# Weight scaling moved from VectorE and ScalarE to GpSimd, and layer 3 of one sample given a shorter share of the schedule, in a four-layer attention network

## The chip, the cores and the metric

The kernel runs on one core of a Trainium2 chip. A core has five engines, each with an instruction queue of its own that is worked off in order: TensorE (PE, matrix products and transposes, with its weight loads listed as PEld), VectorE (DVE), ScalarE (ACT), GpSimd (POOL) and SyncE (SP, which here only issues DMAs). They meet through semaphores. The metric is the device time of one execution in microseconds, as the median of several runs.

## The reference

An input of 16 samples, 64 x 64 tokens of 256 channels, float32, goes through four residual layers. Before each, a group norm over 32 groups of 8 channels is taken, over all tokens of a sample.

```
x = x + L0(gn(x))   # nearest of 1024 code vectors, by distance; the code is added
x = x + L1(gn(x))   # f, g, h = three projections (32, 32, 256 wide); rows of 64 tokens:
                    # out = sigmoid(f g^T) h
x = x + L2(gn(x))   # three projections to one number per token (x0, x1, x2);
                    # sm = softmax over n of x0[n] * x1[m]; gate = sigmoid(x2 . sm);
                    # gate * x
x = x + L3(gn(x))   # linear attention, 4 heads of 32: softmax of q over the head's width,
                    # of k over the tokens; context = k v^T; projection, bias, layer norm
```

A group norm is an affine map of each channel, so its factor can be multiplied into the rows of the next weight, and its mean goes into a bias row. These are the scalings that the change is about.

## The kernel before

Each sample passes through six stages, written as Python generators that yield after small steps:

- `stats0`: statistics of the input for the first norm.
- `stage1`, the search: for each of 32 tiles of 128 tokens PE makes the products with all codes (`pd`, L403), DVE adds the norms and takes the maximum in one instruction (L409), finds its place (L414), and GpSimd adds the code's row by an indirect DMA, the gather (L415). Chunks of four tiles are then transposed back (L378).
- `layer1`: eight chunks of 512 tokens, projections `pfg` (L482) and `ph` (L493), scores, and the weighted sum `po` (L533), added on DVE (L538).
- `rows2`: the three projections of layer 2 to rows (`pr`, L593), written to DRAM and read back spread over all partitions (`x0b`, `x2b`).
- `stage2`, called exps in the schedule: 64 pairs of a 2048-wide exponential on ACT (`ex_s`, L645, with its sum) and a product with `x2b` and its sum on DVE (L648); both operands of the latter lie in the on-chip buffer SBUF. `gate2` then applies the gate (L702, L703).
- `stage3`: layer 3. For eight chunks the projections `pk` (L767) and `pqv` (L786), the running maximum of k (`nkm`, L770), the softmax of q with help of GpSimd (L808, L760), the context `pc` (L811, gathered on DVE in L813); then eight chunks of output with the variance (`pz` L863, `qz` L865), the deviation (`pdv`, `qo` L882) and the final products (L908 to L918).

The stages of neighbouring samples overlap. A list at the end of the kernel gives each stage of each sample a start and a length in units of one search, called a period here; a heap draws the generators' next steps by these times, and that order of recording is the priority. `LEN3` gives the length of layer 3 by the number of samples that come after (`left`); a sample not listed gets 1.0. A scheduler below then lays out each engine's queue from this order. Blocks under `tc.high_priority(offset=URGENT)` are pulled forward in it: the end of each norm and what hangs on it.

`gn_finish` (L276 and after) is the end of a norm: the groups' means on PE, squares and copies on ACT (L288, L293, L295), then on GpSimd the power of -0.5 (L296, on `scale`) and the product `nbias` (L298). For layer 2 a subtraction for a later layer (`xm_`, L688) stands before them in GpSimd's queue. What hangs on `scale`: in `layer1` the weights `wfg_n` (2 x 64 columns, ACT) and `wh_n` (2 x 256, DVE), then the bias products `pb` (L464) and `prow_h` (L163) on PE; in `rows2` two copies of 12 columns into `wrow_n` (ACT, L574), then PE's `pbr` (L579) and ACT's `brow_n` (L583); in `stage3` `wk_n` (2 x 128, ACT) and `wqv_n` (2 x 256, DVE), then `prow_qv` (L163). The helper `scaled` issues one instruction for each half of the channels, L306 on ACT or L308 on another engine.

Of the kernel before, what the change touches and what calls it, by code (L numbers as in the profile page):

```python
# [12 lines left out]
AF = mybir.ActivationFunctionType  # L13
ALU = mybir.AluOpType
AX = mybir.AxisListType

P = 128
# [17 lines left out]
LAG2 = 0.17  # L35
LAG3, LENG = 0.06, 0.8
LAG4 = 0.04
LEN3 = {0: 0.4, 1: 0.33, 2: 0.37}
FILL = ((0.05, 0.95, 2), (1.0, 1.27, 3), (1.4, 1.58, 2))
EARLY = sum(n for _, _, n in FILL)  # L40

# [2 lines left out]
def kernel(  # L44
# [7 lines left out]
    nc = tc.nc  # L52
# [17 lines left out]
    def bank(name):  # L70
        return ps_m.tile([P, 512], F32, tag="pm", name=name)
# [60 lines left out]
    def busy(t, n):  # L132

        for _ in range(n):
            nc.tensor.matmul(
                t[:, :512], lhsT=ones3, rhs=ones3.unsqueeze(1).to_broadcast([P, 4, P]), start=True, stop=True,
                skip_group_check=True,
            )
# [6 lines left out]
    def put_row(dst, v, weight, tag, plus=None, idle=0):  # L145

        v3 = small.tile([P, NK, PARTS], F32, tag="v3", name=f"v3_{tag}")
        nc.scalar.copy(v3, v.unsqueeze(2).to_broadcast([P, NK, PARTS]))
        pb = bank(f"prow_{tag}")
        busy(pb, idle)  # L150
        row = pb[:PARTS, :C]
        weight(row, v3, plus)

        for n in range(PARTS - 1):
            top = small.tile([PARTS, C], BF16, tag="ptop", name=f"top_{tag}_{n}", bufs=1)
            nc.scalar.copy(top, row)
            nc.tensor.matmul(row, lhsT=below[:, n, :], rhs=top, start=False, stop=True, skip_group_check=True)
        nc.scalar.copy(dst[0:PARTS, :], row)

    def by_weight(w):  # L160
        def make(out, v3, plus):
            for k in range(NK):
                nc.tensor.matmul(  # L163
                    out, lhsT=v3[:, k, :], rhs=w[:, k, :], start=(k == 0), stop=(plus is None and k == NK - 1),
                    skip_group_check=True,
                )
            for k in range(NK if plus is not None else 0):
                nc.tensor.matmul(
                    out[:, k * P : (k + 1) * P], lhsT=plus[:, k, :], rhs=ident, start=False, stop=(k == NK - 1),
                    skip_group_check=True,  # L170
                )
        return make
# [61 lines left out]
    wrow_raw = const.tile([P, NK, 4], F32, name="wrow_raw")  # L234
# [66 lines left out]
    def scaled(t, scale, engine):  # L301

        for k in range(NK):
            v = t[:, k]
            if engine is nc.scalar:
                nc.scalar.activation(v, v, AF.Copy, scale=scale[:, k : k + 1])  # L306
            else:
                engine.tensor_scalar(v, v, scale[:, k : k + 1], None, ALU.mult)  # L308
# [4 lines left out]
    def stats0(b):  # L313
        tag = f"s0_{b}"
        st = stats_tile(0, f"st_{tag}")
        src = xT[b].rearrange("(k p) n -> p k n", p=P)
        for ch in range(NCHUNK):
            xt = xb.tile([P, NK, CW], F32, tag="xb", name=f"xs_{tag}_{ch}")
            nc.sync.dma_start(out=xt, in_=src[:, :, ch * CW : (ch + 1) * CW])
            chunk_stats(st, xt, ch)  # L320
            yield 1.5
        with tc.high_priority(offset=URGENT):
            norm0[b] = gn_finish(st, "n0", b)
        yield 2
# [116 lines left out]
    def layer1(b):  # L441
        tag = f"l1_{b}"
        scale, nmean, _ = norm1.pop(b)
        x1 = x1_d.pop(b)
        wfg_n = wts.tile([P, NK, 2 * CK], F32, tag="wfg_n", name=f"wfg_{tag}")
        load_wfg(wfg_n)
        wh_n = wts.tile([P, NK, C], F32, tag="wh_n", name=f"wh_{tag}")
# [8 lines left out]
        load(1)  # L456
        with tc.high_priority(offset=URGENT):

            scaled(wfg_n, scale, nc.scalar)
            scaled(wh_n, scale, nc.vector)  # L460
            pb = bank(f"pb_{tag}")
            for n in range(4):
                for k in range(NK):
                    nc.tensor.matmul(  # L464
                        pb[n * CK : (n + 1) * CK, 0:1], lhsT=wfg_n[:, k, (n // 2) * CK : (n // 2 + 1) * CK],
                        rhs=nmean[:, k : k + 1], start=(k == 0), stop=(k == NK - 1),
                    )
            bfg_n = small.tile([P, 1], F32, tag="bfg_n", name=f"bfg_{tag}")
            nc.scalar.activation(bfg_n, pb[:, 0:1], AF.Identity, bias=bfg)
            put_row(h_row, nmean, by_weight(wh_n), f"h_{tag}", plus=bh3)  # L470
# [96 lines left out]
    def rows2(b):  # L567
        tag = f"r2_{b}"
        scale, nmean, _ = norm2[b]
        with tc.high_priority(offset=URGENT):  # L570
            pb = bank(f"pbr_{tag}")
            busy(pb, 3)
            for k in range(NK):
                nc.scalar.activation(  # L574
                    wrow_n[:, k, :].rearrange("p (j n) -> p j n", n=32)[:, :, 0:3],
                    wrow_raw[:, k : k + 1, 0:3].to_broadcast([P, 4, 3]), AF.Copy, scale=scale[:, k : k + 1],
                )
            for k in range(NK):
                nc.tensor.matmul(  # L579
                    pb[:, 0:1], lhsT=wrow_n[:, k, :], rhs=nmean[:, k : k + 1], start=(k == 0), stop=(k == NK - 1)  # L580
                )
            brow_n = small.tile([P, 1], F32, tag="brow_n", name=f"brow_{tag}")
            nc.scalar.activation(brow_n, pb[:, 0:1], AF.Identity, bias=brow)  # L583
        x01 = small.tile([P, NT, 2], F32, tag="x01", name=f"x01_{tag}", bufs=2)
        rd = dram.tile([3, 2, 4, CW], F32, tag="rows", name=f"rows_{tag}", bufs=3)
        for h in range(2):
            pr = bank(f"pr_{tag}_{h}")
            for j in range(4):
                xt = xb.tile([P, NK, CW], F32, tag="xb", name=f"xr_{tag}_{h}_{j}")
                nc.sync.dma_start(out=xt, in_=x2_d[b][4 * h + j])  # L590
                part = slice(32 * j, 32 * j + 32)
                for k in range(NK):
                    nc.tensor.matmul(  # L593
                        pr[part, :], lhsT=wrow_n[:, k, part], rhs=xt[:, k, :], start=(k == 0), stop=(k == NK - 1)
                    )
            rows = s1p.tile([P, CW], F32, tag="t4", name=f"rows_{tag}_{h}", bufs=3)
            nc.scalar.activation(rows, pr, AF.Identity, bias=brow_n)
            for n in range(3):
                nc.scalar.dma_start(out=rd[n, h], in_=rows[n : n + 97 : 32, :])
            pt = bank(f"prt_{tag}_{h}")  # L600
            for t in range(CH):
                nc.tensor.transpose(pt[:, t * P : (t + 1) * P], rows[:, t * P : (t + 1) * P], ident)
            nc.vector.tensor_copy(
                x01[:, 16 * h : 16 * h + 16, :].rearrange("p (j t) n -> p j t n", t=CH),
                pt.rearrange("p (t j n) -> p j t n", j=4, n=32)[:, :, :, 0:2],
            )
            yield 4
        rows_d[b] = x01, rd, [spread_rows(rd, b, 0)]

    def spread_rows(rd, b, h):  # L610

        x0b = s2p.tile([P, TOK // 2], F32, tag="x0b", name=f"x0b_{b}_{h}", bufs=2)
        x2b = s2p.tile([P, TOK // 2], F32, tag="x2b", name=f"x2b_{b}_{h}", bufs=2)
        for dst, n in ((x0b, 0), (x2b, 2)):
            nc.sync.dma_start(
                out=dst, in_=rd[n : n + 1, h, :, :].rearrange("o j n -> o (j n)").to_broadcast([P, TOK // 2])
            )
        return x0b, x2b
# [98 lines left out]
    def stage3(b):  # L717
# [3 lines left out]
        scale, nmean, xm_ = norm3.pop(b)  # L721
        wk_n = wts.tile([P, NK, P], F32, tag="wk_n", name=f"wk_{tag}")
        nc.sync.dma_start(out=wk_n, in_=w_src[:, :, 1, :])
        wqv_n = wts.tile([P, NK, 2 * P], F32, tag="wqv_n", name=f"wqv_{tag}")
        nc.sync.dma_start(out=wqv_n[:, :, 0:P], in_=w_src[:, :, 0, :])
        nc.sync.dma_start(out=wqv_n[:, :, P:], in_=w_src[:, :, 2, :])
        with tc.high_priority(offset=URGENT):
            scaled(wk_n, scale, nc.scalar)
            scaled(wqv_n, scale, nc.vector)
            put_row(qv_row, nmean, by_weight(wqv_n), f"qv_{tag}")  # L730
        yield 4

# [213 lines left out]
    def task(stage, ready, length, gen, total):  # L946
        start = max(ready, free.get(stage, 0.0))
        free[stage] = start + length
        tasks.append((start, length, gen, total))
        return start + length  # L950

    for b in range(nb):
# [9 lines left out]
        else:  # L962
            end = task("exps", end + LAG2, 0.65, stage2(b, NCHUNK), 200)
        task("layer3", end + LAG4, LEN3.get(left, 1.0), stage3(b), 160)
    for _ in stats0(0):
# [45 lines left out]
```

## Time and profile before

| what | value |
|---|---|
| median of three runs | 5653.41 us (5650.06 to 5654.34) |
| the profiled execution | 5630.88 us, span 5629.1 us |
| mean granted clock of PE | 0.964 |
| scalings on DVE (L308) | 64, 0.35 to 0.36 us each |
| scalings on ACT (L306) | 32 of wfg at 0.338 us, 32 of wk at 0.389 us |
| scalings on ACT (L574) | 32 at 0.294 us |
| GpSimd, busiest lines | gathers L415 1140.5 us, L808 249.7, L760 198.0, L874 172.3 |
| exps on DVE (L648) | 1024, mean 2.34 us |

Times in the views are microseconds from the first instruction of the profiled execution. A line of the timeline gives the start, the duration, engine, source line, operation, what it writes and reads with its shape, and in brackets how long the engine had been idle before it and what ended that. In the list for a source line the three numbers are the shortest, median and longest duration in ns, and below stand what its engine waited for (total us, times). Engines run ahead of each other through buffers, so an idle engine is a cost only where it is the one that the others wait for. The profiled execution is one of many and is 22.5 us shorter than the median of the runs.

### The profile page before, as it was taken

The page shows a single profiled execution, that of the slowest core. Times are in us where ns is not written, and L with a number is a line of the kernel's source. Part 1 is how long each engine was busy: PE and PEld are TensorE (multiplying, and loading weights), DVE is VectorE, ACT ScalarE, POOL GpSimd, SP SyncE. Part 2 cuts the span into 40 slices and gives each one's busy share as a digit, 9 for nine tenths or more (in the row PEclk, how much of TensorE's full clock was granted, in tenths as well). Part 3 has the DMA queues.
Part 4 walks back from the last instruction along what each step waited for, and adds up shares of the span by engine and source line. Part 5 has one row for each costly group of instructions (what it writes and reads, how often), then busy time and mean ns, then how long its engine had stood idle before and what let it go on. Part 6 is the DMA issues. An engine that isn't in the chain of part 4 may idle for free. (4 is left out here: it accounts for less than half of the span.)

```text
span 5629.1 us, 76169 instructions
## 1 busy us (share of the span) xinstructions
PE 5138.9 (91%) x26927; PEld 3174.3 (56%) x26927; DVE 5068.5 (90%) x7186; ACT 4560.2 (81%) x6642; POOL 1832.7 (33%) x1076
## 2 busy tenths in 40 slices
PE   7977989989999999999999999999999999997788
PEld 3533446545656556565655656565565656665566
DVE  7579789899999999999999999999999999988982
ACT  4468589788879888887988888798888979888873
POOL 2223223323333333433333343333334334321231
PEclk9988999999999999999999999999999999998889
DMA  8552744755665757566575756757575675745643
GB/s 253 173 184 73 227 132 123 226 166 174 192 214 150 235 156 228 184 204 221 164 251 152 230 175 207 228 155 247 154 226 183 204 226 152 231 152 193 203 158 121
DMA packets 521366, 1059.26 MB, mean 188 GB/s; under 512 B 52505, under 2 KB 266393, under 8 KB 512793
## 3 DMA queue, kind: packets, MB, share of 16 engines
q1 hardware_dynamic: 406288, 885.11, 46.9%
q0 software_dynamic: 73728, 67.14, 8.5%
q10 hardware_dynamic: 40968, 102.13, 4.7%
q8 instruction: 214, 3.51, 0.3%
q14 instruction: 168, 1.37, 0.1%
HBM read 751.18 MB, written 303.04 MB: 187 GB/s over the span
## 5 line engine op out<-in xcount | busy, mean ns | idle before, releaser
L648 DVE CUSTOM_DVE_ANT_0 ex_s<-ex_s,x2b 128x2048 f32<-128x2048 f32 x1024 | 2388.3, 2340 | 55.7 <-ACT ex_s L645 54.2
L645 ACT ACTIVATE ex_s<-x0b,nmax_s,x_r 128x2048 f32<-128x2048 f32 x1024 | 2138.5, 2089 | 40.3 <-DVE num_s L648 28.8
L403 PE MATMUL pd_s<-e,xn_s 128*128 128x512 f32 x4096 | 1971.2, 615 | 54.0 <-DVE m L409 41.8
L415 POOL DMA_INDIRECT xc_s<-in_emb_rows,i_s x512 | 1140.5, 2228 | 1778.4 <-DVE i_s L414 1274.6
L403 PEld LDWEIGHTS pd_s<-e,xn_s 128*128 128x128 f32 x4096 | 747.3, 196 | 786.9 <-issue 666.4
L409 DVE CUSTOM_DVE_ANT_0 nn_s<-pd_s,nn_s 128x1024 f32<-128x1024 f32 x512 | 620.1, 1213 | 114.4 <-PE pd_s L403 72.3
L414 DVE FIND_INDEX8 i_s<-m,nn_s 128x8 uint32<-128x1024 f32 x512 | 622.7, 1217 | 0.0
L398 ACT ACTIVATE nn_s<-ne,nx_s 128x1024 f32<-128x1024 f32 x512 | 583.3, 1145 | 40.7 <-DVE nx_s L369 24.8
L493 PE MATMUL ph_l<-wh_l,xt_l 128*128 128x256 f32 x2048 | 522.2, 392 | 33.8 <-DVE m L409 27.5
L786 PE MATMUL pqv_s<-wqv_s,xk_s 128*128 128x256 f32 x2048 | 489.3, 381 | 0.0
L493 PEld LDWEIGHTS ph_l<-wh_l,xt_l 128*128 128x128 f32 x2048 | 383.2, 194 | 144.9 <-issue 72.7
L786 PEld LDWEIGHTS pqv_s<-wqv_s,xk_s 128*128 128x128 f32 x2048 | 389.4, 191 | 120.7 <-issue 60.8
L808 POOL TENSOR_TENSOR qv_s<-qv_s,qm_s 128x512 f32<-128x512 f32 x128 | 249.7, 1951 | 580.6 <-DVE qm_s L807 316.0
L874 POOL TENSOR_TENSOR lrs_s<-lrs_s,mhalf 128x4 f32<-128x4 f32 x128 | 172.3, 1346 | 662.7 <-ACT lrs_s L873 655.3
L760 POOL TENSOR_TENSOR qv_s<-qv_s,qd_s 128x512 f32<-128x512 f32 x128 | 198.0, 1547 | 378.2 <-DVE qd_s L759 249.5
L378 PE MATMUL pt_s<-ident,xc_s 128*128 128x128 f32 x1024 | 163.0, 288 | 127.6 <-DMA xc_s<-in_emb_rows,i_s 102.3
L533 PE MATMUL po_l<-blk,h_l 128*128 128x128 f32 x2048 | 272.5, 282 | 3.2 <-DVE m L409 3.2
L533 PEld LDWEIGHTS po_l<-blk,h_l 128*128 128x128 f32 x2048 | 251.2, 194 | 36.8 <-issue 19.9
L914 PE MATMUL pxo_s<-wctx_s,qo_s 128*128 128x256 f32 x1024 | 267.8, 385 | 0.0
L767 PE MATMUL pk_s<-xk_s,wk_s 128*128 128x512 f32 x512 | 252.5, 616 | 1.4 <-DMA xk_s<-x_g 1.4
L378 PEld LDWEIGHTS pt_s<-ident,xc_s 128*128 128x128 f32 x1024 | 123.2, 147 | 191.7 <-DMA xc_s<-in_emb_rows,i_s 120.4
L919 ACT COPY y_s<-pxo_s 128x512 f32<-128x512 f32 x256 | 147.6, 580 | 103.2 <-PE pxo_s L918 102.4
(206 smaller groups left out, 7372.6 us busy)
## 6 DMA issues: line engine op xcount, KB each, us to landing
xs_s<-in_xT SPq DMA_DIRECT2D x128, 512.0 KB
xt_s<-in_xT SPq DMA_DIRECT2D x128, 512.0 KB
xc_s<-in_x SPq DMA_DIRECT2D x128, 512.0 KB
x_s<-xt_s ACTq DMA_DIRECT2D x128, 512.0 KB
xt_l<-x_s SPq DMA_DIRECT2D x128, 512.0 KB
x_l<-xt_l SPq DMA_DIRECT2D x128, 512.0 KB
xr_r<-x_l SPq DMA_DIRECT2D x128, 512.0 KB
xg_g<-x_l SPq DMA_DIRECT2D x128, 512.0 KB
```

What stands on the lines that cost most here:

```text
L378: nc.tensor.transpose(pt[:, t * P : (t + 1) * P], xc[ch][:, t, k * P : (k + 1) * P], ident)
L398: nc.scalar.activation(nn, ne2, AF.Identity, bias=nx2[ch][:, t : t + 1])
L403: nc.tensor.matmul(pd[:, cols], lhsT=xn[ch][:, k, t * P : (t + 1) * P], rhs=e2[:, k, cols], start=(k == 0), stop=(k == NK - 1),)
L409: nc.vector.tensor_tensor_reduce(out=nn, in0=pd, in1=nn, scale=1.0, scalar=-3.0e38, op0=ALU.add, op1=ALU.max, accum_out=m8[:, 0:1],)
L414: nc.vector.max_index(i8, m8, nn)
L415: nc.gpsimd.indirect_dma_start(out=xc[ch][:, t, :], out_offset=None, in_=emb_rows, in_offset=bass.IndirectOffsetOnAxis(ap=i8[:, 0:1], axis=0),
L493: nc.tensor.matmul(ph[:, t, :], lhsT=X[:, k, t * P : (t + 1) * P], rhs=wh_n[:, k, :], start=(t % 2 == 0 and k == 0), stop=False, skip_grou ...
L533: nc.tensor.matmul(po[:, m : m + P], lhsT=h[:, t, k * P : (k + 1) * P], rhs=at[:, t, :, :].rearrange("p r i -> p (r i)"), start=True, stop ...
L645: nc.scalar.activation(ex, x0b, AF.Exp, bias=nmax[:, T : T + 1], scale=x01[:, T, 1:2], accum_out=den[:, h, T : T + 1])
L648: nc.vector.tensor_tensor_reduce(out=ex, in0=ex, in1=x2b, scale=1.0, scalar=0.0, op0=ALU.mult, op1=ALU.add, accum_out=num[:, h, T : T + 1],)
L786: nc.tensor.matmul(pqv[:, j, :], lhsT=xt[:, k, t * P : (t + 1) * P], rhs=wqv_n[:, k, :], start=(j == 0 and k == 0), stop=False, skip_group ...
L914: nc.tensor.matmul(px[:, j, :], lhsT=qT[:, t * P : (t + 1) * P], rhs=wctx[:, 1, :], start=False, stop=False, skip_group_check=True,)
```

## The change

All weight scalings go to GpSimd, as one tensor-by-scalar product for each half of the channels; and the table of layer 3's lengths gets an entry for the thirteenth sample (three samples come after it), 0.7 of a period.

```diff
-LEN3 = {0: 0.4, 1: 0.33, 2: 0.37}
+LEN3 = {0: 0.4, 1: 0.33, 2: 0.37, 3: 0.7}
...
-            scaled(wfg_n, scale, nc.scalar)
-            scaled(wh_n, scale, nc.vector)
+            scaled(wfg_n, scale, nc.gpsimd)
+            scaled(wh_n, scale, nc.gpsimd)
...
-                nc.scalar.activation(
+                nc.gpsimd.tensor_scalar(
                     wrow_n[:, k, :].rearrange("p (j n) -> p j n", n=32)[:, :, 0:3],
-                    wrow_raw[:, k : k + 1, 0:3].to_broadcast([P, 4, 3]), AF.Copy, scale=scale[:, k : k + 1],
+                    wrow_raw[:, k : k + 1, 0:3].to_broadcast([P, 4, 3]), scale[:, k : k + 1], None, ALU.mult,
                 )
...
-            scaled(wk_n, scale, nc.scalar)
-            scaled(wqv_n, scale, nc.vector)
+            scaled(wk_n, scale, nc.gpsimd)
+            scaled(wqv_n, scale, nc.gpsimd)
```

What is computed stays the same. By the schedule's times layer 3 of that sample starts at 15.83 periods as before and ends at 16.53 and not at 16.83; the next sample's layer 3 starts at 16.83 in both.

## Prediction

> **What bounds the kernel now.** I read the page's busy line first, then busy time by stretch, then the groups of the scaling line, then the timeline around one sample's three scalings. The columns of the stretches are: from and to, length, then busy time and instructions of PE, PEld, DVE, ACT, POOL, then clock and DMA.
>
> ```profile
> PE 5138.9 (91%) x26927; PEld 3174.3 (56%) x26927; DVE 5068.5 (90%) x7186; ACT 4560.2 (81%) x6642; POOL 1832.7 (33%) x1076
> ```
> ```profile
> 4918.00:5076.00 158.00, 143.40 (x889) 103.04 (x888) 140.87 (x193) 138.32 (x214) 36.31 (x24) 0.95 0.48 154
> 5076.00:5200.00 124.00, 93.56 (x453) 61.42 (x454) 109.10 (x134) 100.74 (x144) 20.24 (x15) 0.85 0.57 199
> ...
> 1987.00:4951.00 2964.00, 2811.22 (x15128) 1751.35 (x15127) 2827.36 (x3985) 2548.89 (x3721) 1057.80 (x592) 0.99 0.64 199
> ```
>
> From 1987 to 4951 us (ends of the search's matmuls, L403, of the seventh and the sixteenth sample) nine samples pass, 329 us each. PE and DVE are both busy 95% of it (2811 and 2827 of 2964): they take turns in waiting for each other, so time freed on one counts only until the other ends the next wait. Later, in 4918 to 5200, where the change of layer 3's pace falls, PE goes from 91% to 75% while DVE stays at 88 to 89%.
>
> ```profile
> L308 DVE TENSOR_SCALAR wh_l<-wh_l,gn_s_n x32: 336/350/394, 193.2 to 4972.8; 128x256 f32<-128x256 f32 x32
> ...
>   POOL gn_s_n L296: 50.5, 31
> ```
>
> This line and its twin for wqv_s (x32, 0.36 us) are 64 scalings on DVE, and before 31 of the 32 pairs DVE sat idle for GpSimd's power of -0.5 (L296), 50.5 us in all. That looks like a prize of 50.5 + 64 x 0.35 = 73 us. The timeline says why it isn't.
>
> ```profile
> 3981.97 2.23 DVE L648 CUSTOM_DVE_ANT_0 ex_s<-ex_s,x2b 128x2048 f32<-128x2048 f32 x1
> 3982.03 3.07 POOL L808 TENSOR_TENSOR qv_s<-qv_s,qm_s 128x512 f32<-128x512 f32 x1 [6.87 <-issue]
> ...
> 3985.06 1.04 POOL L760 TENSOR_TENSOR qv_s<-qv_s,qd_s 128x512 f32<-128x512 f32 x1
> ...
> 3985.76 1.05 PE L811 MATMUL pc_s<-qv_s,ek_s 128*128 128x128 f32 x8
> ...
> 3986.84 0.65 DVE L308 TENSOR_SCALAR wh_l<-wh_l,gn_s_n 128x256 f32<-128x256 f32 x2 [2.63 <-POOL gn_s_n L296]
> ...
> 3987.41 0.34 DVE L813 SCALAR_TENSOR_TENSOR ctx_s<-ctx_s,al_s,pc_s 128x128 f32<-128x128 f32 x1
> ```
>
> Two things are to be seen. DVE's next instruction, L813, reads pc_s, whose matmuls end at 3986.81. And L808 and L760, the same shape on GpSimd, take 3.07 us when begun under ex_s (L648) and 1.04 us without: **GpSimd stands still while DVE runs ex_s.** The norm of the second layer shows the same at a two-column operation:
>
> ```profile
> 3904.33 2.28 DVE L648 CUSTOM_DVE_ANT_0 ex_s<-ex_s,x2b 128x2048 f32<-128x2048 f32 x1
> 3904.39 2.27 POOL L688 TENSOR_TENSOR xm_g<-bet,gn_nm_n 128x2 f32<-128x2 f32 x1 [1.28 <-ACT gn_nm_n L295]
> ...
> 3906.62 0.72 POOL L296 TENSOR_TENSOR gn_s_n<-gn_s_n,mhalf 128x2 f32<-128x2 f32 x1
> 3907.38 0.50 ACT L574 ACTIVATE wrow_n<-wrow_raw,gn_s_n 128x12 f32<-128x12 f32 x2 [2.03 <-POOL gn_s_n L296]
> 3907.43 0.19 POOL L298 TENSOR_TENSOR gn_nb_n<-gn_nm_n,gn_s_n 128x2 f32<-128x2 f32 x1
> 3907.75 2.27 DVE L648 CUSTOM_DVE_ANT_0 ex_s<-ex_s,x2b 128x2048 f32<-128x2048 f32 x1
> ```
>
> **Prices of the new instructions.** The trace has no scaling on GpSimd. Below, each costs what L298 costs with two columns, 0.19 us. Above, a line from L298 (0.19 at 2 columns) to the free L760 (1.04 at 512, two tensors read): 12 columns 0.21, 64 0.29, 128 0.40, 256 0.61. The new ones read one tensor, so the upper end is generous; I take it, as these are the same shapes. wfg and wh are then 2 x 0.29 + 2 x 0.61 = 1.8 us, wk and wqv 2.0, wrow 0.4 (lower ends 0.8, 0.8, 0.4). Any of them begun under ex_s waits up to 2.2 us more. Before them in GpSimd's queue stands L298 (0.19), behind them the gathers L415; the weights themselves are long there (the last wk load was issued at 5433.9, its scaling began at 5501.9). The Trainium skill (GPSIMD Engine Reference, Engine selection) advises against the move: ordinary elementwise work belongs on VectorE, though it grants GpSimd about the same rate where one tensor is read. Taken at that word the 256-column scaling would cost DVE's own 0.35 us in place of 0.61, the pairs 1.3 us at most, and the sum below would fall by 1 us or less; no run here shows which.
>
> **Layer 1's weights (wfg, wh), in a steady period.** Removed: DVE's 2.63 idle and 0.65 busy, ACT's 0.68 busy and 1.02 idle. In the order of the changed program L813 follows ex_s on DVE, waiting for PE's pc_s, ended at 3986.81: the same idle under another name. L813 starts near 3986.95 and not 3987.41: **0.46 us gained, not 3.3.** PE never paused there. The new scalings end near 3986.81 + 0.2 + 1.8 = 3988.8, or 3991 if the last is caught by an ex_s; PE wants wh at 3992.1 (L163, one matmul earlier in the new order than 3992.58). Covered; without that cover PE would wait. The gather behind them began at 3991.45: covered as well.
>
> **Layer 3's weights (wk, wqv).** In 1987 to 4951 PE takes them up more than 20 us after they are scaled, so the price on GpSimd is hidden (the next one there, near 3898, comes 11 us later). DVE gains its wait for L296 (5.0 us in seven samples of 2322 to 4633: 0.7) and 0.6 busy: **1.3 us**, on DVE alone.
>
> **Layer 2's rows (wrow).** Now the scalings stand behind L298 on GpSimd, which ends at 3907.62: the first runs to about 3907.8, the second meets the ex_s of 3907.75 and would end near 3910.1. PE's second L579 would wait till then in place of about 3907.95: **2.2 us lost** on PE (idle 1.72 us here already), on ACT (L583 waits for it, the exps behind) and on the rows, which the next sample's exps wait for. The phase is held, as L688 is released by the end of one ex_s and the next comes 1.21 us later; seven samples (2583 to 4566 us) show L688 at 2.27 us. Two more have L298 itself caught: I count nine.
>
> **Sum, steady.** Gains 12 x (0.46 + 1.3) = 21 us of DVE time, of which PE's part of the waits lets through half by my judgement: -11. Loss 9 x 2.2 = 20, on a chain that PE, ACT and the exps all hang on, seven tenths through: +14. Together **+3 us**.
>
> **Start.** At 499.6 and 747.3 the layer 1 chain has no cover: PE sat idle for it 1.3 and 0.9 us, and DVE has two ex_s next. Caught by both, the scalings come 4.4 us late; half through, twice: **+4 us**.
>
> **Layer 3 of sample 12.** Its start is unchanged (15.83 periods), its end goes from 16.83 to 16.53. The work is the same. I summed before's mean durations along both programs' orders: when its last deviation (L882) is done, DVE has 352 us left, against 318; PE's last pr_r (L593) has 342 against 373 left. So layer 3 is drawn into 4918 to 5076, where PE has 15 us to spare, and 5076 to 5200, with 30 to spare, gets emptier. DVE's work before the end of the next-to-last exps is the same, 286 us remaining against 287. The moved DMAs (layer 3's loads xk and xo and stores of y on SP, qT on ACT's queue) now pass the gate's loads of sample 13 and layer 1's of sample 15 on SP; the DMA engines are at 0.48 to 0.57 there, so I charge them nothing, and a late xt_l would cost its wait on PE, counted in the upper bound. For the pace itself I take 0, bounds -10 (most of DVE's 15 us of waits in 5076 to 5200 go) and +15 (PE's extra wait earlier is passed on in full). One consequence I do price: layer 3 of sample 13 now finds PE free, and DVE's first nkm (L770) stands 9.5 us of DVE work behind the norm, where it stood 39. Before that nkm come PE's statistics to pk, 7.4 us in before (5159.88 to 5167.27), 1.6 more on GpSimd, and the two casts that now precede pk, about 4: 13 us, without an ex_s in the way, and the DVE work there is nothing but ex_s. DVE waits 3.5 to 8: **+6 us** where DVE sets the end.
>
> **End.** Sample 15's wqv is on the path: pow to the end of the fourth prow_qv is 2.4 us now, later 0.2 + 2.0 + 0.9 = 3.1, +0.7. Sample 0's layer 1, with no exps yet and PE idle for it: wh ready 2.0 us after the power and not 0.7, +1.3. **+2 us.**
>
> Sum: 3 + 4 + 6 + 2 = +15. The profiled execution took 5630.9 us (span 5629.1); 5646. The median of the runs is 22.5 above it: **5668 us.** With the bounds of the pace, the largest unknown, its own range is 5658 to 5683.
>
> **Rivals.** *Faster (0.26):* the second wrow scaling slips in before ex_s and DVE's gains carry: 12 x -1.76 = -21, start and end +6, tail -10 + 3.5: 5632. For it speaks that 0.05 us decides; against, that ex_s follows ex_s wherever DVE is full. *Nothing (0.14):* gains and catches cancel, 5654: PE was busy at both weight changes. *Every scaling caught by its own ex_s (0.10):* four of wfg and wh take 9.2 us, against 5.3 of cover; 4 us of PE a period, 11 times, on top of the sum: 5712. Against it: at 3987 DVE has L813 and L409 first, and L808 ran its 1.05 us beside such work. It decides once DVE's ex_s come earlier than GpSimd's L296.
>
> **How the numbers follow.** Forecast 0.50, of which 0.09 lies within 0.2% (11 us, about what a measurement of this kernel can tell). Slower 0.41 + 0.10 = 0.51, same 0.09 + 0.14 = 0.23, faster 0.26. The range takes in the faster case's time and nearly the caught one's: 5628 to 5706.
>
> **What would show it.** Right: DVE's L813 idle for pc_s about 2.5 us a period; the second wrow scaling near 2.2 us and PE's L579 idle near 4; DVE idle at nkm near 5150 to 5180. Wrong: L308 and L574 on GpSimd all under 0.7 us with L579 idle under 2, or periods under 328 us; or PE waiting at prow_h_l, which makes the caught case.

## The result, and the profile after

The changed kernel took 5681.53 us (median of 14 runs, 5655.13 to 5707.56), the kernel before 5650.95 in the runs between them. The ratio is 1.0062 with a 95% interval of 1.0045 to 1.0079: **some 35 us slower** (25 to 45). All comparisons go by such ratios; the two medians alone differ by 30.6 us. One run of the kernel before took 8676 us and one of an experiment below 7092, and both stay out of the ratios. The forecast was 5668 us and slower, so its direction held and its size was too small. The profiled execution took 5670.3 us, 39 more than that of before.

The page's busy line of the changed kernel, and the stretches that answer to those of before (from and to, length, then busy time and instructions of PE, PEld, DVE, ACT, POOL, then granted clock, share of the DMA engines, GB/s). The third is again from the end of the seventh to the end of the sixteenth search, which lie at 1989.24 and 4986.58 now:

```profile
PE 5155.1 (91%) x26927; PEld 3187.3 (56%) x26927; DVE 5053.8 (89%) x7122; ACT 4537.5 (80%) x6546; POOL 1986.8 (35%) x1236
```
```profile
4918.00:5076.00 158.00, 143.90 (x790) 94.75 (x788) 129.22 (x189) 124.65 (x195) 49.73 (x31) 0.96 0.51 165
5076.00:5200.00 124.00, 99.44 (x607) 70.13 (x599) 103.46 (x120) 99.64 (x137) 27.45 (x19) 0.86 0.63 220
...
1989.24:4986.58 2997.34, 2836.56 (x15166) 1767.82 (x15165) 2823.45 (x3962) 2541.83 (x3679) 1137.22 (x685) 0.98 0.63 197
```

The nine steady samples take 2997 us and not 2964. DVE's work fell a little, as was wanted (2823 from 2827, though more of layer 3 lies within). PE is *busy* for longer, 2837 against 2811, and its granted clock went from 0.99 to 0.98. Not all of it is the 38 matmuls more: the search's own, of which there are as many in both stretches, show it in the groups of PE (busy us, mean ns of one, idle time before them), here before and after the change:

```profile
L403 PE MATMUL pd_s<-e,xn_s 128*128 128x512 f32 x2305 | 1100.5, 607 | 14.3 <-DVE m L409 12.8 <-DVE xt_l L538 1.5
L403 PE MATMUL pd_s<-e,xn_s 128*128 128x512 f32 x2305 | 1122.2, 617 | 12.6 <-DVE m L409 11.1 <-DVE xt_l L538 1.5
```

The same 2305 matmuls were busy for 1100.5 us, 607 ns each, and now take 22 us more for equal work. That is easily passed over; the experiments come back to it.

The groups of the two scaling lines after the change (shortest, median and longest ns):

```profile
L308 POOL TENSOR_SCALAR wfg_l<-wfg_l,gn_s_n x32: 432/444/2570, 192.1 to 5007.8; 128x64 f32<-128x64 f32 x32
L308 POOL TENSOR_SCALAR wh_l<-wh_l,gn_s_n x32: 912/917/2661, 193.0 to 5009.1; 128x256 f32<-128x256 f32 x32
L308 POOL TENSOR_SCALAR wk_s<-wk_s,gn_s_n x32: 592/606/2702, 790.2 to 5536.3; 128x128 f32<-128x128 f32 x32
L308 POOL TENSOR_SCALAR wqv_s<-wqv_s,gn_s_n x32: 912/917/4844, 791.3 to 5537.8; 128x256 f32<-128x256 f32 x32
L574 POOL TENSOR_SCALAR wrow_n<-wrow_raw,gn_s_n x32: 306/322/2422, 294.1 to 5149.7; 128x12 f32<-128x12 f32 x32
```

256 columns take 0.92 us where DVE took 0.35; the longest of each group are those begun under ex_s. And the timeline around layer 2's rows, at the sample that the prediction used (start, duration; in brackets the engine's idle time before):

```profile
3921.74 1.58 POOL L688 TENSOR_TENSOR xm_g<-bet,gn_nm_n 128x2 f32<-128x2 f32 x1 [0.75 <-ACT gn_nm_n L295]
...
3923.29 0.72 POOL L296 TENSOR_TENSOR gn_s_n<-gn_s_n,mhalf 128x2 f32<-128x2 f32 x1
3924.10 0.19 POOL L298 TENSOR_TENSOR gn_nb_n<-gn_nm_n,gn_s_n 128x2 f32<-128x2 f32 x1
3924.27 2.59 POOL L574 TENSOR_SCALAR wrow_n<-wrow_raw,gn_s_n 128x12 f32<-128x12 f32 x2
3924.40 2.28 DVE L648 CUSTOM_DVE_ANT_0 ex_s<-ex_s,x2b 128x2048 f32<-128x2048 f32 x1
...
3924.65 0.38 PE L579 MATMUL pbr_r<-gn_nm_n,wrow_n 128*128 128x1 f32 x2 [1.39 <-POOL wrow_n L574]
...
3926.92 0.38 PE L579 MATMUL pbr_r<-gn_nm_n,wrow_n 128*128 128x1 f32 x2 [1.89 <-POOL wrow_n L574]
...
3927.16 4.52 PE L403 MATMUL pd_s<-e,xn_s 128*128 128x512 f32 x6
3927.34 0.26 ACT L583 ACTIVATE brow_r<-pbr_r,brow 128x1 f32<-128x1 f32 x1 [4.75 <-PE pbr_r L579]
```

As forecast: the first scaling of 12 columns slips in (0.3 us), the second meets the ex_s of 3924.40, and the pair takes 2.59 us. PE waits twice and ACT 4.75 us. The waits over the nine samples (us in total, times, longest) show the same; the first line is of the kernel before, the others are of the changed one:

```profile
PE pbr_r L579 <- ACT wrow_n L574: 14.5, 9, 1.7
...
DVE ex_s L648 <- ACT ex_s L645: 50.7, 41, 3.8
ACT brow_r L583 <- PE pbr_r L579: 41.3, 9, 4.9
...
PE pbr_r L579 <- POOL wrow_n L574: 30.2, 17, 3.4
DVE nn_s L409 <- ACT nn_s L398: 28.1, 34, 3.1
DVE ctx_s L813 <- PE pc_s L811: 22.9, 16, 4.0
```

In the kernel before, PE waited 14.5 us there for wrow_n, DVE 29.7 for the exps of ACT and 16.4 for L398, and DVE's 23.7 us before the scaling of wh are now the 22.9 before L813.

### The profile page after: what moved, and what is told of

It is laid out like the page before. It is cut to its first block, busy times and chain, and to the rows that moved or that the text cites. A ratio compares the mean times of both kernels' runs of the same rounds, so it can differ in the third digit from the quotient of the medians.

```text
span 5668.6 us, 76211 instructions
## 1 busy us (share of the span) xinstructions
PE 5155.1 (91%) x26927; PEld 3187.3 (56%) x26927; DVE 5053.8 (89%) x7122; ACT 4537.5 (80%) x6546; POOL 1986.8 (35%) x1236
## 5 line engine op out<-in xcount | busy, mean ns | idle before, releaser
L648 DVE CUSTOM_DVE_ANT_0 ex_s<-ex_s,x2b 128x2048 f32<-128x2048 f32 x1024 | 2387.9, 2339 | 79.3 <-ACT ex_s L645 78.8
L403 PE MATMUL pd_s<-e,xn_s 128*128 128x512 f32 x4096 | 1990.1, 620 | 47.9 <-DVE m L409 35.4
L415 POOL DMA_INDIRECT xc_s<-in_emb_rows,i_s x512 | 1103.2, 2155 | 1705.5 <-DVE i_s L414 1245.3
L403 PEld LDWEIGHTS pd_s<-e,xn_s 128*128 128x128 f32 x4096 | 754.2, 197 | 785.8 <-issue 681.0
L398 ACT ACTIVATE nn_s<-ne,nx_s 128x1024 f32<-128x1024 f32 x512 | 583.2, 1145 | 39.4 <-DVE nx_s L369 24.0
L351 ACT ACTIVATE sq_s<-xt_s,first 128x512 f32<-128x512 f32 x256 | 200.1, 806 | 37.5 <-DMA x0b<-rows_r 24.1
```

The costliest lines, as they stand in the source:

```text
L398: nc.scalar.activation(nn, ne2, AF.Identity, bias=nx2[ch][:, t : t + 1])
L403: nc.tensor.matmul(pd[:, cols], lhsT=xn[ch][:, k, t * P : (t + 1) * P], rhs=e2[:, k, cols], start=(k == 0), stop=(k == NK - 1),)
L415: nc.gpsimd.indirect_dma_start(out=xc[ch][:, t, :], out_offset=None, in_=emb_rows, in_offset=bass.IndirectOffsetOnAxis(ap=i8[:, 0:1], axis=0),
L648: nc.vector.tensor_tensor_reduce(out=ex, in0=ex, in1=x2b, scale=1.0, scalar=0.0, op0=ALU.mult, op1=ALU.add, accum_out=num[:, h, T : T + 1],)
```

## The experiments

Each kernel was timed in turn with the kernel before on one chip. All ratios are to that kernel, whose median was 5640 to 5644 us there; 0.1% is 5.6 us. "Clock lost" is the mean over a kernel's runs of span x (1 - mean granted clock). It also counts the clock in stretches in which PE had nothing to do, so only differences of it are used.

| kernel | ratio | 95% interval |
|---|---|---|
| layer 3's length alone | 0.9999 | 0.9984 to 1.0015 |
| all scalings, old length | 1.0077 | 1.0056 to 1.0097 |
| wk and wqv alone | 0.9984 | 0.9971 to 0.9996 |
| layer 2's rows alone | 1.0065 | 1.0044 to 1.0085 |
| all scalings but the rows | 1.0010 | 0.9993 to 1.0026 |
| wfg and wh alone | 1.0028 | 1.0012 to 1.0044 |
| rows in one instruction | 1.0020 | 1.0006 to 1.0034 |
| rows, PE's second wait filled | 1.0045 | 1.0031 to 1.0060 |
| wk and wqv, PE's wait shortened | 0.9991 | 0.9975 to 1.0007 |
| wfg and wh from the fourth sample | 1.0008 | 0.9997 to 1.0019 |
| wfg and wh in the first three | 1.0021 | 1.0003 to 1.0040 |
| the change without its losing parts | 0.9973 | 0.9959 to 0.9987 |

### The change taken apart

The two traces had put 20 of the 39 us ahead of the last search and 16 more within it, where layer 3 of the thirteenth sample lies. That was read as a cost of the shorter length (theory A).

```diff
-LEN3 = {0: 0.4, 1: 0.33, 2: 0.37}
+LEN3 = {0: 0.4, 1: 0.33, 2: 0.37, 3: 0.7}
```

> The kernel before with only the new entry of 0.7 in the table of layer 3's lengths; every scaling stays on its old engine. Theory A (the loss in the tail, about 16 us between the start of the last search and its end, is the shorter layer 3 itself, drawn into a stretch where PE is full): +8 to +20 us on the kernel before, the last search some 10 us or more later. Rival (the pace costs nothing, and the tail only inherits late scalings): -5 to +5 us.

Measured: 0.9999, -1 us (-9 to +8). Of theory A's +8 to +20 only the lowest edge is left.

The same from the other side: the changed kernel with the table of before.

```diff
-LEN3 = {0: 0.4, 1: 0.33, 2: 0.37, 3: 0.7}
+LEN3 = {0: 0.4, 1: 0.33, 2: 0.37}
```

> All scalings on GpSimd, layer 3's lengths as in the kernel before. Theory A: the scalings are worth about +20 us, +15 to +28 with the end's wqv; the delay at the start of the last search (+20 us in the changed kernel) stays and does not grow to +36 behind it. Rival (the pace costs nothing): the whole +35 to +39 us. Rival (it is the pace alone): -5 to +5 us.

Measured: 1.0077, +43 us (32 to 55), no less than the whole change. The delay within the last search belongs to the scalings or to the one profiled execution, not to the length.

```diff
-            scaled(wk_n, scale, nc.scalar)
-            scaled(wqv_n, scale, nc.vector)
+            scaled(wk_n, scale, nc.gpsimd)
+            scaled(wqv_n, scale, nc.gpsimd)
```

> The kernel before with only wk and wqv scaled on GpSimd. Theory A (wk and wqv are wanted 20 us later, so that their price is hidden, and DVE and ACT gain): -10 to +2 us; of it about -12 in the steady part at most, +2 to +6 at the last sample, where wqv is on the path. Rival (each scaling on GpSimd costs what it is slower, 0.91 against 0.35 us for 256 columns, wherever it stands): 2 x 0.56 us a sample and its wait under ex_s, +10 us or more.

Measured: 0.9984, -9 us (-16 to -2). This part gains, though each scaling is slower: in the steady samples nobody waits for it. (Where PE does wait, at the fourteenth sample for 5.94 us and at the last for 3.32, the gain is larger than the loss.)

Then the rows alone: the two L574 on GpSimd as in the change, all else as before.

> The kernel before with only the layer 2 rows' two scalings (12 columns) on GpSimd. Theory A (the second is caught by ex_s, 2.2 us on PE, ACT and the rows): its duration about 2.3 us in a third of the 32 lines or more, PE's wait for wrow_n about 3.3 us a sample against 1.7, and +12 to +22 us. Rival (layer 1's weights are what costs the time, the rows are as fast on GpSimd, 0.31 us against 0.29 free): -3 to +5 us.

Measured: 1.0065, +37 us (25 to 48). **Two instructions of 12 columns a sample cost as much as the whole change.** That is also more than theory A's 12 to 22. PE waited 33.6 us at L579 over nine samples where it had waited 14.5: 2.1 us a sample, or 34 over all 16 if nothing of it were hidden.

### The catch

Both halves in one instruction, otherwise as the rows alone:

```diff
-            for k in range(NK):
-                nc.scalar.activation(
...
+            nc.gpsimd.tensor_tensor(
+                out=wrow_n.rearrange("p k (j n) -> p k j n", n=32)[:, :, :, 0:3],
+                in0=wrow_raw[:, :, 0:3].unsqueeze(2).to_broadcast([P, NK, 4, 3]),
+                in1=scale.unsqueeze(2).unsqueeze(3).to_broadcast([P, NK, 4, 3]), op=ALU.mult,
+            )
```

> The rows' scalings on GpSimd as in the run with them alone, but both halves in one instruction of 24 columns, so that no second one stands before ex_s. Theory B (the catch): the instruction takes 0.3 to 0.5 us in most samples, PE waits about 1.7 us a sample as before, time -4 to +8 us on the kernel before. Rival (it is the way over GpSimd, behind L298 in its queue, not the catch): +20 us or more, as with two instructions (+37).

The group of the new line in its trace:

```profile
L573 POOL TENSOR_TENSOR wrow_n<-wrow_raw,gn_s_n x16: 217/222/228, 291.8 to 5105.2; 128x24 f32<-128x24 f32 x16
```

None of the 16 is caught. Measured: 1.0020, +11 us (3 to 19), just above theory B's +8 and under the rival's +20. The same work on the same engine at the same place in its queue costs about a third of what it cost in two instructions; the rest of the loss was the catch. The new form is also the cheaper one, 0.22 us for both halves where two free ones took 0.62, but 16 x 0.4 = 6 us cannot make up the 26. What the +11 are was not taken further. PE's wait for wrow_n is 56 us in that trace and 41 in the trace of before, and two samples show where: at 1608.87 and 1936.77 PE waits 3.26 us for wrow_n, with a mean clock of 0.57 over the 8 us from 1608 and from 1936, where in the kernel before L579 follows without a wait at a clock of 1.00.

### What the wait costs

Why 37 us? With the rows alone, the nine samples have 2844 us of PE's busy time against 2811 for the same matmuls; those of the search take 619 ns each and not 607. The timeline of PE around one of the waits, and the granted clock there (length, busy time and instructions of PE, clock, DMA):

```profile
3269.26 1.10 PE L403 MATMUL pd_s<-e,xn_s 128*128 128x512 f32 x2
3272.33 0.38 PE L579 MATMUL pbr_r<-gn_nm_n,wrow_n 128*128 128x1 f32 x2 [1.97 <-POOL wrow_n L574]
3274.60 0.58 PE L579 MATMUL pbr_r<-gn_nm_n,wrow_n 128*128 128x1 f32 x2 [1.88 <-POOL wrow_n L574]
3275.04 5.35 PE L403 MATMUL pd_s<-e,xn_s 128*128 128x512 f32 x6
```
```profile
3268.00:3272.00 4.00, 2.36 (x13) 1.00 0.72 210
3272.00:3276.00 4.00, 1.78 (x5) 0.66 0.08 33
3276.00:3280.00 4.00, 4.00 (x6) 0.50 0.24 33
```

Six L403 take 5.35 us: the clock has fallen to half behind the two waits. It does so in all nine samples: over the 8.5 us from the first L579 the mean clock is 0.60 to 0.62 in eight of them and 0.80 in one. Theory C: the wait is paid twice, once as idle time and once as matmuls at half the clock. The test adds work to PE: products that nobody reads, between the two L579, in the second wait.

```diff
             for k in range(NK):
                 nc.tensor.matmul(
                     pb[:, 0:1], lhsT=wrow_n[:, k, :], rhs=nmean[:, k : k + 1], start=(k == 0), stop=(k == NK - 1)
                 )
+                for _ in range(8 if k == 0 else 0):
+                    nc.tensor.matmul(
+                        pb[:, 256:384], lhsT=wrow_n[:, 0, :], rhs=ident, start=True, stop=True, skip_group_check=True,
+                    )
```

> The rows' two scalings on GpSimd, and PE gets eight products of 128 columns that nobody reads between the two L579, which fill its second wait for wrow_n (about 1.9 us). Theory C (the wait leads PE's granted clock to fall to 0.5 for some 6 us behind it, which costs as much again as the wait): with the work added the half-clock rows behind L579 go, and the time falls from +37 to between +8 and +24 us. Rival (the wait alone, 2.2 us and what hangs on it, is the loss): +35 us or more, as work is added and none is taken away.

The same place in its trace (the added products are its L583):

```profile
3281.23 1.11 PE L403 MATMUL pd_s<-e,xn_s 128*128 128x512 f32 x2
3284.30 0.38 PE L579 MATMUL pbr_r<-gn_nm_n,wrow_n 128*128 128x1 f32 x2 [1.97 <-POOL wrow_n L574]
3284.55 2.03 PE L583 MATMUL pbr_r<-ident,wrow_n 128*128 128x128 f32 x16
3286.57 0.38 PE L579 MATMUL pbr_r<-gn_nm_n,wrow_n 128*128 128x1 f32 x2
3286.81 2.82 PE L403 MATMUL pd_s<-e,xn_s 128*128 128x512 f32 x6
```

The catch is still there (the second L579 stands 2.3 us behind the first in both), and the same six L403 take 2.82 us. This is one of three samples of the nine in which the clock stays at 1.00 over 8.5 us; in the six others it is 0.80; the first wait, of 1.97 us, is still there. Over the nine samples the search's matmuls are back at 609 ns. Here they are with the rows alone, then with the filled wait:

```profile
L403 PE MATMUL pd_s<-e,xn_s 128*128 128x512 f32 x2306 | 1126.0, 619 | 14.6 <-DVE m L409 13.1 <-DVE xt_l L538 1.5
L403 PE MATMUL pd_s<-e,xn_s 128*128 128x512 f32 x2305 | 1103.9, 609 | 14.6 <-DVE m L409 13.2 <-DVE xt_l L538 1.5
```

Measured: 1.0045, +25 us (17 to 34), a hair above theory C's +24; the interval overlaps that of the rows alone (25 to 48), so the times by themselves only lean to it. The clock tells the two apart: it lost 219 us a run with the filled wait, 218 in the kernel before beside it, and 241 with the rows alone (220 before, beside it). The six runs of the rows alone have mean clocks of 0.955 to 0.959, the five with the filled wait 0.959 to 0.963. So by this count, of the rows' +38 us in mean span (5679.3 against 5641.3), **22 us are clock** (241.4 - 219.5) and **16 are waits and what hangs on them**. The 22 are an upper figure and the 16 a lower one, as over the runs of the kernel before a span grew by only 0.6 to 0.9 us for each us of clock lost. The filled wait gave the clock back and yet only some 15 us of mean span (+23, 5665.6 against 5642.2): the rest of the span is 23 us longer than before and not 16, so the filler itself seems to cost some 6.

The same idea on the good part: wk and wqv on GpSimd, and five products ahead of L579 to shorten the 1.7 us that PE waits in the kernel before.

```diff
             busy(pb, 3)
+            for _ in range(5):
+                nc.tensor.matmul(
+                    pb[:, 256:384], lhsT=ident, rhs=nmean[:, 0:1].to_broadcast([P, P]), start=True, stop=True,
+                    skip_group_check=True,
+                )
```

> The kernel before with wk and wqv scaled on GpSimd (-9 us by itself) and, on PE, five products of 128 columns that nobody reads ahead of L579, which shorten PE's wait for the rows' factors from about 1.7 us to 0.7. Theory C (a wait of PE there lets the granted clock fall behind it, and the runs of one kernel differ by how often it does): the clock lost is 5 to 15 us less than in the kernel before, and the time -12 to -25 us on it. Rival (only waits of 3 us and more cost clock, and the kernel before has none here): -9 to +5 us, as the added work gains nothing.

Measured: 0.9991, -5 us (-14 to +4), no better than without the products, and short of theory C's -12. The clock does gain what was expected, 11 us less lost (205 against 216), but the rest of the span is 6 us longer (5427.5 against 5421.5). The added products (ten matmuls a sample, one every 0.11 us: some 18 us of PE over 16 samples) are likely in the way: in the trace of wk and wqv alone PE doesn't wait for wrow_n at L579 in seven of the 16 samples, and waits 1.14 to 1.57 us in the others. That a filler pays only where it fits into the wait is a reading of this and not shown.

### Layer 1's weights

All scalings on GpSimd but the rows, which go back to ScalarE, with layer 3's lengths of before (the edit of the rows is shown against the changed kernel, its first line only):

```diff
-                nc.gpsimd.tensor_scalar(
+                nc.scalar.activation(
...
```

> wfg, wh, wk and wqv on GpSimd, layer 2's rows on ScalarE as before, layer 3's lengths as before. Theory B (nearly all of the loss is the rows' second scaling caught by ex_s): -14 to +5 us on the kernel before, where the same with the rows on GpSimd took +43. Rival (the prices of layer 1's and layer 3's scalings make up a good part): +12 us or more.

Measured: 1.0010, +6 us (-4 to +15), against +43 with the rows: theory B rather than its rival, though 1 us above its range. As wk and wqv gain 9, something costs more than forecast.

```diff
-            scaled(wfg_n, scale, nc.scalar)
-            scaled(wh_n, scale, nc.vector)
+            scaled(wfg_n, scale, nc.gpsimd)
+            scaled(wh_n, scale, nc.gpsimd)
```

> The kernel before with only wfg and wh scaled on GpSimd. Theory B: DVE's wait for the power becomes one for pc_s and half a microsecond a sample is gained, PE's start costs up to 4: -8 to +6 us. Rival (the 0.91 us of a 256-column scaling, some of them caught by ex_s, reach PE at prow_h): +10 us or more.

Measured: 1.0028, +16 us (7 to 25). Theory B missed it. Its clock lost no more than before (219 against 218). To see where it lies, the samples were parted, first with GpSimd from the fourth on:

```diff
+            eng = nc.gpsimd if b > 2 else None
-            scaled(wfg_n, scale, nc.scalar)
-            scaled(wh_n, scale, nc.vector)
+            scaled(wfg_n, scale, eng or nc.scalar)
+            scaled(wh_n, scale, eng or nc.vector)
```

> wfg and wh on GpSimd from the fourth sample on, in the first three as before. Theory D (layer 1's +16 us come from the start, where PE stands still for the whole chain of scalings): -6 to +5 us on the kernel before. Rival (a scaling caught by ex_s in each steady period costs PE at prow_h): +8 to +16 us.

Measured: 1.0008, +5 us (-2 to +11). Then with `b <= 2` in its place:

> wfg and wh on GpSimd in the first three samples alone. Theory D: +9 to +18 us on the kernel before, with PE idle for about 5 us ahead of pb in the second and third sample where it was idle about 1. Rival (the steady periods): -2 to +5 us.

Measured: 1.0021, +12 us (2 to 23). **Most of layer 1's cost seems to lie in the first three samples.** The two intervals overlap; the traces speak for it too, as PE's waits for wfg there go from 1.5, 1.3 and 0.9 us to 1.9, 5.2 and 4.6, and from the fourth sample on no wait for wfg over 0.5 us is left in the changed kernel. The timeline at the second sample, first a line of the kernel before, then of this run (the inserted line moves the numbers behind it up by one, L648 to L649, L464 to L465):

```profile
500.03 0.54 PE L464 MATMUL pb_l<-gn_nm_n,wfg_l 128*32 128x1 f32 x10 [1.31 <-ACT wfg_l L306]
...
501.02 1.64 POOL L296 TENSOR_TENSOR gn_s_n<-gn_s_n,mhalf 128x2 f32<-128x2 f32 x1 [8.38 <-ACT v_h_l L148]
...
502.07 2.28 DVE L649 CUSTOM_DVE_ANT_0 ex_s<-ex_s,x2b 128x2048 f32<-128x2048 f32 x1
502.73 1.67 POOL L298 TENSOR_TENSOR gn_nb_n<-gn_nm_n,gn_s_n 128x2 f32<-128x2 f32 x1
...
504.28 2.28 DVE L649 CUSTOM_DVE_ANT_0 ex_s<-ex_s,x2b 128x2048 f32<-128x2048 f32 x1
504.39 2.93 POOL L308 TENSOR_SCALAR wfg_l<-wfg_l,gn_s_n 128x64 f32<-128x64 f32 x2
...
506.95 0.27 PE L465 MATMUL pb_l<-gn_nm_n,wfg_l 128*32 128x1 f32 x2 [5.24 <-POOL wfg_l L308]
507.30 1.82 POOL L308 TENSOR_SCALAR wh_l<-wh_l,gn_s_n 128x256 f32<-128x256 f32 x2
```

One ex_s follows the other, and the queue of GpSimd is caught again behind the power (L296, 1.64 us in both kernels): L298 takes 1.67 us, 0.20 in the kernel before, and the scalings of wfg 2.93. PE stands idle for 5.24 us, 1.31 in the kernel before. At the fourth sample, around 1063, PE has layer 3's products to do.

### A version that beats both

The changed kernel with the rows back on ScalarE and with wfg and wh on GpSimd only from the fourth sample on:

```diff
+            late = nc.gpsimd if b > 2 else None
-            scaled(wfg_n, scale, nc.gpsimd)
-            scaled(wh_n, scale, nc.gpsimd)
+            scaled(wfg_n, scale, late or nc.scalar)
+            scaled(wh_n, scale, late or nc.vector)
...
-                nc.gpsimd.tensor_scalar(
+                nc.scalar.activation(
...
```

> The changed kernel with its two losing parts taken back: layer 2's rows on ScalarE, and wfg and wh on GpSimd only from the fourth sample on; wk, wqv and layer 3's length as changed. If the parts add up (0.9984 for wk and wqv, 1.0008 for the late wfg and wh, 0.9999 for the length): 0.999, -5 us on the kernel before, within -14 to +4. Rival (the parts are not independent, each shift of the order costs clock somewhere else): +8 us or more.

Measured: 5624.51 us against 5641.89, 0.9973, **-15 us** (-23 to -7). It beats both kernels. The expected -5 us lies just outside the interval. Whether the parts together do better than their sum isn't shown, as the intervals of the three parts are 6 to 9 us wide to each side. The clock has little share in the gain (219 lost, 221 before). The shorter length may be worth more once the scalings have moved, which no run parts.

## Why the prediction was partly right

- **"GpSimd stands still while DVE runs ex_s": shown** by the rows in one instruction, which the ex_s no longer catches. In the changed kernel's trace 146 of 159 instructions of the scalings, norms and layer 3 on GpSimd that begin under an ex_s end behind it; in the 13 others it is ex_s that took longer, 4.3 to 5.1 us. The Trainium skill (Trainium Architecture — The Big Picture, "What this means for kernel authors") calls the port pair that the two engines share an exclusive lock and not a split of bandwidth. The trace agrees: 0.32 us for a free scaling of 12 columns, 2.42 for the longest caught one.
- **"The second meets the ex_s", nine samples: shown.** In 12 samples of the changed kernel's trace the pair takes 2.6 us or more; in 11 of them the second scaling is the one caught, in the sixteenth the first. Of the nine steady samples eight are caught.
- **"Loss 9 x 2.2 = 20, seven tenths through: +14": the term that failed.** The rows cost +37. The waits and what hangs on them, 16 us, are near the forecast's 14; the other 22, by the count above, are PE's clock, which the prediction had no term for, though the page of the profile has a row for it. This gap is about as large as the forecast's whole error (+35 against +15).
- **Prices of the scalings: too low by a third** (0.61 us forecast at 256 columns, 0.92 measured). The line was drawn through TENSOR_TENSOR rows, and these are TENSOR_SCALAR: 0.32 us at 12 columns, where a TENSOR_TENSOR of 24 takes 0.22. The Trainium skill's word (GPSIMD Engine Reference, Engine selection) that GpSimd keeps about the line rate with one tensor would have put 0.35, further off; the measurement decides. In wk and wqv, behind cover, the higher price cost nothing that shows.
- **wfg and wh, "the same idle under another name": right** in the steady part. L813 waits 22.9 us for pc_s where L308 waited 23.7, and from the fourth sample on the move costs -2 to +11 us. The rival of 5712, in which every scaling is caught and PE waits at prow_h, did not come: PE waited for wh there 2.7 us in the whole changed kernel.
- **wk and wqv, "the price is hidden", 1.3 us of DVE a period, half of it through: right**, -9 us measured against 12 x 1.3 x 0.5 = 8.
- **Start +4: likely too small.** Layer 1 in the first three samples cost +12 us, but its interval (2 to 23) takes in the forecast. PE's waits for wfg grew by 3.9 us in the second sample (5.24 against 1.31) and 3.7 in the third (4.61 against 0.91), 7.6 in all; "half through" put 4.4 us for the two.
- **Layer 3's length, pace 0: right** (-9 to +8). The idle time behind the +6, 3.5 to 8 us of DVE, came, most of it under another name. In the changed kernel:

```profile
5183.94 1.91 PE L163 MATMUL prow_qv_s<-wqv_s,v_qv_s 128*3 128x256 f32 x4 [7.06 <-POOL wqv_s L308]
...
5185.89 0.36 ACT L156 CAST top_qv_s<-prow_qv_s 3x256 bf16<-3x256 f32 x1 [5.62 <-PE prow_qv_s L163]
...
5188.37 2.29 DVE L648 CUSTOM_DVE_ANT_0 ex_s<-ex_s,x2b 128x2048 f32<-128x2048 f32 x1 [5.76 <-ACT ex_s L645]
...
5192.76 0.69 DVE L770 TENSOR_REDUCE nkm_s<-pk_s 128x1 f32<-128x512 f32 x1 [2.09 <-PE pk_s L767]
```

  Ahead of nkm DVE waits only 2.09 us, but just before, 5.76 us for ACT's exponential, which stood in ACT's queue behind a cast that waited 5.62 us for PE's products with wqv. Together that is 7.85 us; in the kernel before DVE was idle 0.19 us between the scalings at 5162 and its nkm at 5179. The forecast had "without an ex_s in the way"; the two scalings of wk met one and took 3.29 us. What these waits cost isn't shown: wk and wqv alone, with a wait of 5.94 us for wqv at the same sample, still gain 9 us.
- **Steady sum +3: wrong**; the parts measured alone make 37 - 9 + 5 = +33, nearly all of it the rows.
- **The time: partly luck.** 5681.5 us lies within the forecast's 5658 to 5683, but that range was made for the pace of layer 3, which cost nothing; what filled it was the loss of the rows.
- **End +2:** not tested by itself. PE waits 3.31 us for the last sample's wqv in the changed kernel.

The measured parts add up, within their intervals: 65 + 28 - 16 - 1 = 76 hundredths of a per cent, against 77 for all scalings and 62 (45 to 79) for the change.

## What to carry to other kernels

An engine that shares a path with another is not priced by its free duration: look at what the other engine runs in the microsecond after, and put short steps on the critical chain into one instruction, so that there is no second one to be caught. Price a wait of PE in two parts, the idle time and the matmuls that may run behind it at a lower clock; where the busy time of PE grows at the same number of matmuls, as here from 1100.5 to 1122.2 us, the second part has been paid. A slower engine is a gain for work that nobody waits for (wk, wqv), and a loss for the same work where the pipeline isn't yet full (the first three samples).

## What was not expected of the hardware

PE's clock can fall after pauses shorter than looked for. In the kernel before, one wait of 1.72 us ahead of L579 (3907.74) was enough:

```profile
3904.00:3908.00 4.00, 2.28 (x13) 1.00 0.62 163
3908.00:3912.00 4.00, 4.00 (x10) 0.65 0.00 0
```

PE was busy 2.28 us of the first four and had half the clock for most of the next. But the same wait doesn't always do it. Of seven samples with a wait of 1.72 to 1.73 us the clock fell behind four; here is one that did and one that did not, 6 us each from just before L579:

```profile
2586.00:2592.00 6.00, 5.61 (x18) 0.72 0.25 59
2916.00:2922.00 6.00, 5.16 (x26) 1.00 0.16 21
```

What tells the two apart is open. Two waits of 1.97 and 1.88 us with 0.38 of work between them cost 5.35 - 2.82 = 2.5 us in the six L403 that follow. The Trainium skill (TensorE: Matmul & The Clock Gate, "HAM oscillation — how this bites in real kernels") puts the rule at idle gaps of more than about 3.4 us. Here shorter ones did it, some of the time, so the measurement decides.

The runs of one and the same kernel differ by this clock. Over the kernel before's 29 runs beside the rows in one instruction, spans go from 5625 to 5665 us with mean clocks of 0.965 to 0.959, and span and clock lost go together (correlation 0.84, 0.86 us of span for each us lost; in the other three groups of runs of this kernel 0.76 to 0.84, and 0.60 to 0.81 us).
